# Attention's weight products in three float32r passes instead of seven block products, with every engine's order written out

## The chip, the cores and the metric

The kernel runs on one core of a Trainium2 chip. The metric is the device time of one launch in microseconds, of which the median of several runs is given. TensorE (PE) does the matrix products and writes them to PSUM; VectorE (DVE), ScalarE (ACT) and GpSimd (POOL) work on the data around them; SyncE (SP) issues most of the transfers.

## The reference

The reference is one transformer layer over 4 x 2048 tokens of 256 features in float32: attention within chunks of 32 tokens, then a feed-forward part with 768 hidden features and integer weights.

```python
Q, K, V = x @ W_q.T, x @ W_k.T, x @ W_v.T          # chunks of 32 tokens
S = einsum('bncd,bnkd->bnck', Qc, Kc) * mask       # mask: decay ** (i - j), lower triangle
O = einsum('bnck,bnkd->bncd', S, Vc)
attn = sigmoid(x @ W_g.T) * O @ W_o.T + x
h = layernorm(x + attn)
ffn = (silu(h @ wg.T) * (h @ wu.T)) @ wd.T         # weights: integer / 127
out = layernorm(h + ffn)
```

## The kernel before, in words

The 8192 tokens are cut into 16 blocks of 512 (TB). `W_q.T W_k` is folded once into a matrix m (`make_m`), so a block needs four weight products of 512 tokens by 256 by 256: the gate (g), y = m x, the values (v) and the output projection (o). Scores and values are fp32 products of small pieces (L631, L652). The feed-forward part has six chunks of 128 hidden features (`ffn_up`, L795: fg and fu, each as a float32r high part and an f16 low part, two products per part) and the down projection (`ffn_down`, fdn, L682 or, for the last blocks, chunkwise L858 and L1128).

The four weight products of blocks 1 to 15 (o: 1 to 14) are written in Winograd's form of Strassen: `seven` cuts both operands into quarters and makes seven fp32 products of quarter size instead of eight. The sums of weight quarters are made once (`weight_sums`, POOL), those of token quarters for every block (`token_sums`, POOL, tiles x_sums and go_sums). Four products go first into four banks (p1, p6, p5, p7); ACT copies p1 and p5 out (L505), DVE and POOL build sums of them (L507 to L517); the other three products are accumulated onto three of these banks later (`others`), and ACT and DVE read the quarters out (L524, L530). `feature_major` gives g and y with features on partitions (products of 256 columns), `token_major` gives v and o with tokens on partitions (128 columns).

The loop `for b in range(NB - 2)` works on several blocks at once: the feed-forward part of block b, scores and values and output projection of block n = b + 2, and v, y and g of block m = b + 3. In a steady turn PE does up 0, up 1, scores, up 2, v (first products), up 3, v (rest), values, y (first), up 4, up 5, y (rest), g (first), o (first), g (rest), o (rest), down. The normalised h of block b + 1 is transposed by DVE (`move_h`) and 16 transfers, and split by `split_h`. The layer norm after attention takes the statistics (`moments`, DVE), the root (`root`, ACT, with a table load, and a table load back to silu), a reciprocal on DVE and three small POOL operations (`scale_and_shift`), and `normalize` on ACT.

The order on each engine is that of a planner for instructions left free, and that of the program for those passed to `in_turn` (`tc.keep_in_program_order`). `in_steady_turn` is `in_turn` where the Python flag `steady` is true, which is so for b > 0. Eight PSUM banks are handed out in rotation; the tile pools `sums`, `work` and `xin` have one or two buffers for each tag.

At the head, blocks 0 to 2 have their attention products before the loop begins, and block 0's products are plain fp32 (`attn_gate`, `attn_v`, `attn_y`, `attn_residual`). In block 15 the output projection is also plain fp32 ("pa", L682). A second path for wide integer weights (`wide_block`) is behind a runtime condition and isn't taken with these inputs.

Of the kernel before, what the change touches and what calls it, by code (L numbers as in the profile page):

```python
# [66 lines left out]
HALF = 0.5  # L67
WARM = 512, 512, 128
# [3 lines left out]
def kernel(  # L72
# [130 lines left out]
    def make_m():  # L203
        pm = bank("pm")
        for ec in range(KD):
            for dc in range(KD):
                nc.tensor.matmul(
                    pm[:, ec * D : (ec + 1) * D],
                    lhsT=wq[:, dc, ec * P : (ec + 1) * P],
                    rhs=wk[:, dc, :],  # L210
                    start=(dc == 0),
                    stop=(dc == KD - 1),
                )
        nc.scalar.copy(m_sb.rearrange("p k n -> p (k n)"), pm)
# [3 lines left out]
    nc.scalar.activation(decay, decay, AF.Sigmoid)  # L218
# [10 lines left out]
    power = decay  # L229
    for i in range(CHUNK.bit_length() - 1):  # L230
# [4 lines left out]
        bit = setup.tile([P, CHUNK], F32, tag="bit", name=f"bit_{i}")  # L235
        nc.vector.tensor_copy(bit, bit_int)
        factor = setup.tile([P, CHUNK], F32, tag="factor", name=f"factor_{i}")
        nc.vector.tensor_scalar(factor, bit, -1.0, 1.0, ALU.mult, ALU.add)
        nc.vector.scalar_tensor_tensor(factor, bit, power, factor, ALU.mult, ALU.add)
        nc.vector.tensor_tensor(chunk_mask, chunk_mask, factor, ALU.mult)  # L240
        if i < CHUNK.bit_length() - 2:
            square = const.tile([P, 1], F32, tag=f"power_{i}", name=f"power_{i}")
            nc.vector.tensor_tensor(square, power, power, ALU.mult)
            power = square
    mask = const.tile([P, NG, PAIR], F32, tag="mask", name="mask")
    nc.vector.memset(mask, 0.0)
    for g in range(P // CHUNK):
        rows = slice(g * CHUNK, (g + 1) * CHUNK)
        at = g * CHUNK % PAIR
        nc.vector.tensor_copy(  # L250
            mask[rows, :, at : at + CHUNK],
            chunk_mask[rows, :].unsqueeze(1).to_broadcast([CHUNK, NG, CHUNK]),
        )


# [5 lines left out]
    def integers(w, w_int, name):  # L261
# [6 lines left out]
        for t in both:  # L268
            for i, piece in enumerate(w_int):
                tc.keep_in_program_order(nc.scalar.copy(pieces_of(t, i), piece))  # L270
        return both
# [29 lines left out]
    def in_turn(ins):  # L301
        tc.keep_in_program_order(ins)

# [4 lines left out]
    steady = False  # L308
# [117 lines left out]
    def weight_sums(w, name):  # L426

        a11, a21 = w[:, 0, :P], w[:, 0, P:]
        a12, a22 = w[:, 1, :P], w[:, 1, P:]
# [20 lines left out]
    def feature_major(a, b):  # L450


        def product(i, pb, first, order=free):
# [8 lines left out]
                )  # L462
            )

        return product

    def token_major(a, b):

# [850 lines left out]
```

## Time and profile before

| | us |
|---|---|
| median of 3 runs | 524.97 (523.98 to 525.20) |
| profiled execution: its own time | 525.22 |
| profiled execution: span of the program | 523.6 |
| PE busy | 517.1 |
| DVE, ACT, POOL busy | 327.2, 325.8, 343.3 |
| head: up to the loop's first chunk | 48.8 |
| one steady block | 31.6 |
| block 13 of the loop (b = 13) | 22.8 |

The span runs from the first to the last instruction of the program. In a line of the profile, L813 is a line of the kernel; then come the engine, the operation, and the tiles as out<-in. The records of PE overlap, [...]so their pace is read from the distance of two starts; an fp32 product appears as two records.

### The profile page before, as it was taken

The numbers are of one execution on the slowest core, as the hardware profiler recorded it, in microseconds if no ns is written. First come the engines' busy times: TensorE is split into PE (matmuls) and PEld (weight loads), VectorE is DVE, ScalarE is ACT, GpSimd is POOL, SyncE is SP. The second block draws the span as 40 slices with busy tenths as digits, with TensorE's granted clock in tenths as the row PEclk, the third lists the DMA queues.
The fourth block names the chain that finished last, engine by engine and source line by source line (L and its number), as shares of the span: only waits on it lengthen the run. The fifth ranks groups of instructions, "written<-read, shape, count | busy, mean of one in ns | idle before, by whom it ended". The sixth has DMA issues, their size and how long they took to land.

```text
span 523.6 us, 10506 instructions
## 1 busy us (share of the span) xinstructions
PE 517.1 (99%) x3648; PEld 422.2 (81%) x3648; DVE 327.2 (62%) x867; ACT 325.8 (62%) x646; POOL 343.3 (66%) x475
## 2 busy tenths in 40 slices
PE   9999999999999999999999999999999999999995
PEld 5798887888978789787888878879787888878685
DVE  3868676575655847657475665846657565666554
ACT  3755556475655756667566665756567566666745
POOL 6435875676857768486675866768487685845554
PEclk9999999999999999999999999999999999999999
DMA  7631111212313131121412313131121311102102
GB/s 255 199 109 43 54 51 35 65 41 46 118 28 94 49 114 41 38 85 52 110 42 50 115 25 97 44 111 49 34 89 51 111 42 41 43 20 61 62 21 83
DMA packets 43319, 36.89 MB, mean 70 GB/s; under 512 B 4864, under 2 KB 39168, under 8 KB 43264
## 3 DMA queue, kind: packets, MB, share of 16 engines
q1 hardware_dynamic: 42144, 35.28, 22.9%
q10 hardware_dynamic: 1120, 0.92, 0.6%
q8 instruction: 30, 0.49, 0.4%
q14 instruction: 25, 0.20, 0.1%
HBM read 20.45 MB, written 8.39 MB: 55 GB/s over the span
## 4 chain that ended last, share of the span: by engine, by line
PE 98%; DVE 1%; ACT 0%; issue 0%
PE fg L795 17%; PE fu L795 16%; PE fdn L682 13%; PE p_v L473 9%; PE p_y L455 9%; PE p_g L455 9%; PE p_o L473 8%; PE po L652 5%; PE ps L631 3%; PE fdn L858 2%; PE pa L682 1%; PE pg L571 1%; PE pi L185 1%; PE pv L611 1%; PE py L590 1%; PE fdn L1128 1%
## 5 line engine op out<-in xcount | busy, mean ns | idle before, releaser
L817 POOL TENSOR_TENSOR u_lo<-u,u_hi 128x512 f16<-128x512 f32 (+1 forms) x98 | 122.3, 1256 | 107.0 <-ACT u_hi L816 107.0
L813 DVE SCALAR_TENSOR_TENSOR u<-fu,s 128x512 f32<-128x512 f32 (+1 forms) x98 | 65.2, 677 | 65.5 <-ACT s L803 43.7
L803 ACT ACTIVATE s<-fg 128x512 f32<-128x512 f32 (+1 forms) x98 | 56.6, 584 | 53.5 <-PE fg L795 53.5
L816 ACT CAST u_hi<-u 128x512 fp32r<-128x512 f32 (+1 forms) x98 | 59.5, 610 | 48.5 <-DVE u L813 48.0
L795 PE MATMUL fg<-hT_hi,fg_hi 128*128 128x512 f32 (+1 forms) x196 | 73.8, 458 | 0.0
L795 PE MATMUL fu<-hT_hi,fu_hi 128*128 128x512 f32 (+1 forms) x196 | 60.5, 390 | 0.0
L795 PE MATMUL fg<-hT_lo,fg_lo 128*128 128x512 f16 (+1 forms) x196 | 57.9, 377 | 0.0
L795 PE MATMUL fu<-hT_lo,fu_lo 128*128 128x512 f16 (+1 forms) x196 | 57.4, 375 | 0.0
L682 PE MATMUL fdn<-fd_hi,u_hi 128*128 128x256 f32 x312 | 45.7, 288 | 0.0
L795 PEld LDWEIGHTS fu<-hT_hi,fu_hi 128*128 128x128 f32 x196 | 36.6, 188 | 8.4
L795 PEld LDWEIGHTS fg<-hT_hi,fg_hi 128*128 128x128 f32 x196 | 34.6, 189 | 8.9
L410 ACT ACTIVATE h<-h,shift_h,scale_h 128x256 f32<-128x256 f32 x52 | 27.0, 590 | 22.5 <-POOL shift_h L373 22.5
L682 PEld LDWEIGHTS fdn<-fd_hi,u_hi 128*128 128x128 f32 x312 | 38.9, 189 | 0.3
L682 PE MATMUL fdn<-fd_lo,u_lo 128*128 128x256 f16 x312 | 38.6, 273 | 0.0
L795 PEld LDWEIGHTS <-fu_lo 128*128 128x128 f16 x196 | 19.2, 98 | 22.2
L778 POOL TENSOR_TENSOR hT_lo<-hT,hT_hi 128x512 f16<-128x512 f32 x28 | 35.3, 1279 | 1.2 <-ACT hT_hi L777 1.2
L840 DVE SCALAR_TENSOR_TENSOR r<-fdn,h 128x512 f32<-128x512 f32 x30 | 20.7, 689 | 20.2 <-PE fdn L682 18.1
L795 PEld LDWEIGHTS <-fg_lo 128*128 128x128 f16 x196 | 15.3, 98 | 20.7 <-issue 12.9
L473 PE MATMUL p_v<-v_sums,x_sums 128*128 128x128 f32 x240 | 31.8, 275 | 0.0
L682 PEld LDWEIGHTS <-u_lo 128*128 128x128 f16 x312 | 28.4, 98 | 3.9
L652 PE MATMUL po<-sT,v 128*128 128x128 f32 x256 | 31.2, 275 | 0.0
L455 PE MATMUL p_y<-x_sums,m_sums 128*128 128x256 f32 x120 | 30.8, 379 | 0.0
(211 smaller groups left out, 1154.2 us busy)
## 6 DMA issues: line engine op xcount, KB each, us to landing
x<-in_x_dram SPq DMA_DIRECT2D x16, 512.0 KB, 3.6
xT<-in_xT_dram SPq DMA_DIRECT2D x15, 512.0 KB, 4.2
hT<-sq SPq DMA_DIRECT2D x224, 32.0 KB, 1.9
out_dram<-r SPq DMA_DIRECT2D x13, 512.0 KB, 4.7
out_dram<-r SPq DMA_DIRECT2D x7, 128.0 KB, 1.7
fg_int<-in_ffn_gT_dram SPq DMA_DIRECT2D x3, 256.0 KB, 8.1
fu_int<-in_ffn_uT_dram SPq DMA_DIRECT2D x3, 256.0 KB, 7.1
fd_int<-in_ffn_dT_dram SPq DMA_DIRECT2D x3, 256.0 KB, 5.9
```

Of the source, the lines that this page charges most:

```text
L410: nc.scalar.activation(r[:, g, :], r[:, g, :], AF.Identity, bias=shift[:, g : g + 1], scale=scale[:, g : g + 1],)
L455: nc.tensor.matmul(pb, lhsT=a[i - 1], rhs=b[i - 1], start=first, stop=True, skip_group_check=True,)
L473: nc.tensor.matmul(pb[:, g * P : (g + 1) * P], lhsT=b[i - 1][:, g * P : (g + 1) * P], rhs=a[i - 1], start=first and g == 0, stop=True, ski ...
L652: nc.tensor.matmul(po[:, cols], lhsT=v[:, g, dc * P : (dc + 1) * P], rhs=sT[:, cols], start=True, stop=True,)
L682: nc.tensor.matmul(pb[:, j * D : (j + 1) * D], lhsT=part[:, g * P : (g + 1) * P], rhs=w, start=(i == 0), stop=(i == len(terms) - 1),)
L778: nc.gpsimd.tensor_tensor(in_order[1], whole, in_order[0].bitcast(F32), ALU.subtract)
L795: nc.tensor.matmul(pb, lhsT=w[kind][:, dc, hc * P : (hc + 1) * P], rhs=hT[kind][:, dc, cols], start=(kind == kinds[0] and dc == 0), stop=( ...
L803: order(nc.scalar.activation(s, pg, AF.Silu, scale=SCALE / H_UP))
L813: nc.vector.scalar_tensor_tensor(u, pu, U_UP / H_UP, s, ALU.mult, ALU.mult)
L816: nc.scalar.copy(hi, u)
L817: nc.gpsimd.tensor_tensor(lo, u, hi.bitcast(F32), ALU.subtract)
L840: nc.vector.scalar_tensor_tensor(flat(r, gs), pb, SCALE**2 / U_UP * H_UP, flat(h, gs), ALU.mult, ALU.add)
```

## The change

Each weight product becomes three float32r products. With SHIFT = 2^12, an operand t is split into hi = t * (1 - 0.5/SHIFT), rounded to float32r, lo = t - hi, and a third part, gap. For tokens gap = t - (1 + 1/SHIFT) hi; for weights lo is scaled up by SHIFT after the split and gap = hi - lo. The product is (1 + 1/SHIFT) times the sum of the high and the low product, plus the product of the gaps. `three` runs the high and low pass of both banks, lets ACT multiply each bank by 1 + 1/SHIFT in place in PSUM, and later adds the third pass and finishes the bank: g by ACT's tanh, y by a DVE copy, v by an ACT copy, o by a DVE addition.

The parts of weights are made at the head, hi and the scaling of lo by ACT, lo and gap by POOL. The parts of tokens (x and goT) are made for each block: hi by ACT, lo by POOL, gap by DVE. Block 0 keeps plain fp32. Block 15's output projection is made in three passes too, its third pass between the early and the late terms of the down projection of block 13 (`amid`), and its layer norm goes over POOL's power function and ACT's `normalize`.

`steady` is true from the start, and nearly all instructions of PE, ACT and DVE are pinned to the program's order. The head is rearranged, the casts of the integer weights are spread out between other steps (`cast_fg(0)` and so on), `move_h` comes after chunk 1, the split of h after chunk 5, and in the block without a next one (b = 13) chunk 3 comes behind the values.

```diff
+SHIFT = 2.0**12
+TOP = 1.0 - 0.5 / SHIFT
+WHOLE = 1.0 + 1.0 / SHIFT
...
-    steady = False
+    steady = True
...
+    def weight_parts(w, name, tags):
+        hi, lo = (
+            const.tile([P, KD, D], F32R, tag=tag, name=f"{name}_{kind}")
+            for tag, kind in zip(tags, ("hi", "lo"))
+        )
+        in_turn(nc.scalar.mul(hi, w, TOP))
+        in_turn(nc.gpsimd.tensor_tensor(lo, w, hi.bitcast(F32), ALU.subtract))
+        w_parts[name] = [hi, lo]
+    def weight_up(name):
+        lo = w_parts[name][1]
+        in_turn(nc.scalar.mul(lo, lo.bitcast(F32), SHIFT))
+    def weight_gap(name):
+        hi, lo = w_parts[name]
+        gap = const.tile([P, KD, D], F32R, tag=name, name=f"{name}_gap")
+        in_turn(nc.gpsimd.tensor_tensor(gap, hi.bitcast(F32), lo.bitcast(F32), ALU.subtract))
+        w_parts[name].append(gap)
+    def token_parts(t, name):
+        hi, lo, gap = parts = [
+            sums.tile([P, KD, TB], F32R, tag=f"{name[0]}_{kind}", name=f"{name}_{kind}")
+            for kind in ("hi", "lo", "gap")
+        ]
+        for k in range(KD):
+            whole = hi[:, k, :].bitcast(F32)
+            in_turn(nc.scalar.mul(hi[:, k, :], t[:, k, :], TOP))
+            in_turn(nc.gpsimd.tensor_tensor(lo[:, k, :], t[:, k, :], whole, ALU.subtract))
+        def gaps():
+            for k in range(KD):
+                whole = hi[:, k, :].bitcast(F32)
+                in_turn(nc.vector.scalar_tensor_tensor(
+                        gap[:, k, :], whole, -WHOLE, t[:, k, :], ALU.mult, ALU.add))
+        return parts, gaps
...
+    def three(name, product, finish):
+        banks = [bank(f"p{i}_{name}") for i in range(2)]
+        for i, pb in enumerate(banks):
+            product(i, pb, 0)
+            product(i, pb, 1)
+            in_turn(nc.scalar.mul(pb, pb, WHOLE))
         def others():
...
+            for i, pb in enumerate(banks):
+                product(i, pb, 2)
+                finish(i, pb)
...
+    weight_parts(wg, "wg", ("wg_hi", "wg_lo"))
+    make_mask()
+    weight_parts(wv, "wv", ("wv_hi", "wv_lo"))
+    back_to_silu()
+    sg, gate = attn_gate(0)
+    x_parts, x_gaps = token_parts(xTs[1], "x_1")
...
+    mv = moments(hs[0], "a0", order=in_turn)
+    weight_up("wo")
+    weight_gap("wo")
+    std = root(mv, "a0", HALF, order=in_turn)
+    back_to_silu()
+    v, rest = split_v(2, x_parts)
+    x_gaps()
     goT = attn_values(1, sT_1, v_1, sg_1)
...
         if b:
             normalize(hs[b + 1], *scales_h)
-            moving = move_h(b + 1, hs[b + 1])
-        ffn_up(b, hT, uT, range(0, 1))
+        up_now(b, hT, uT, 0)
         if b == 0:
             g_rest()
-            x_sums = token_sums(xTs[m], f"x_{m}")
-        ffn_up(b, hT, uT, range(1, 2))
+            cast_fd(1)
+            x_parts, x_gaps = token_parts(xTs[m], f"x_{m}")
+        up_now(b, hT, uT, 1)
+        if b:
+            moving = move_h(b + 1, hs[b + 1])
         sT = attn_scores(n, yT)
...
         if more:
-            v_next, v_rest = split_v(m, x_sums)
-        multiply = ffn_up(b, hT, uT, range(3, 4), held=True)
-        if more:
+            v_next, v_rest = split_v(m, x_parts)
+            up_now(b, hT, uT, 3)
             v_rest()
...
         goT = attn_values(n, sT, v, sg)
...
+        go_parts, go_gaps = token_parts(goT, f"go_{n}")
         if more:
-            go_sums = token_sums(goT, f"go_{n}")
-            y_next, y_rest = split_y(m, x_sums)
-        ffn_up(b, hT, uT, range(4, KH))
+            y_next, y_rest = split_y(m, x_parts)
+        else:
+            up_now(b, hT, uT, 3)
+            normalize(r_before, *scales_out)
+            store(b - 2, r_before)
+        up_now(b, hT, uT, 4)
+        go_gaps()
+        up_now(b, hT, uT, 5)
+        hTs[b + 1] = split_h(b + 1, moving)
...
             y_rest()
-            sg_next, g_rest = split_gate(m, x_sums)
-            hs[n], out_rest = split_out(n, go_sums)
+            sg_next, g_rest = split_gate(m, x_parts)
+            hs[n], out_rest = split_out(n, go_parts)
             g_rest()
             mv_h = out_rest()
             ahead = y_next, v_next, sg_next
-            hTs[b + 1] = split_h(b + 1, moving)
+            if m + 1 < NB:
+                x_parts, x_gaps = token_parts(xTs[m + 1], f"x_{m + 1}")
             std_h = root_in_turn(mv_h, of_h, f"h_{b}")
             if b:
                 mv_before, std_before = mv_out, root_in_turn(mv_out, of_out, f"out_{b}")
             back_to_silu()
...
             def between():
-                return scale_and_shift(mv_h, std_h, of_h, f"h_{b}")
+                scales = scale_and_shift(mv_h, std_h, of_h, f"h_{b}")
+                if m + 1 < NB:
+                    x_gaps()
+                return scales
...
         else:
-            hs[n] = attn_residual(n, goT)
-            mv_h = moments(hs[n], f"a{n}", order=in_turn)
             std_out = root_in_turn(mv_out, of_out, f"out_{b}")
-            hTs[b + 1] = split_h(b + 1, moving)
-            std_h = root_in_turn(mv_h, of_h, f"h_{b}")
             back_to_silu()
+            hs[n], out_rest = split_out(n, go_parts)
             scales_out = scale_and_shift(mv_out, std_out, of_out, f"out_{b}")
             normalize(r_before, *scales_out)
             store(b - 1, r_before)
...
-            inverse(std_h, slice(0, NG), HALF)
-            for g in range(NG):
-                scaled(hs[n], g, mv_h, std_h)
-            r_out, mv_out, _ = ffn_down(b, uT, hs.pop(b), chunkwise=True)
+            def amid():
+                return iterated_scale_and_shift(out_rest(), (HALF, 1.0), f"h_{n}")
...
+            r_out, mv_out, scales_h = ffn_down(
+                b, uT, hs.pop(b), chunkwise=True, amid=amid
+            )
+            normalize(hs[n], *scales_h)
             scales_out = iterated_scale_and_shift(mv_out, of_out, f"out_{b + 1}")
```

## The prediction

> **What bounds the kernel now.** I read the page's head and chain first, then the chain in order of time over one steady block, then the engine shares of that block, and last the queues of ScalarE (ACT) and VectorE (DVE) in order of time.
>
> ```profile
> span 523.6 us, 10506 instructions
> PE 517.1 (99%) x3648; PEld 422.2 (81%) x3648; DVE 327.2 (62%) x867; ACT 325.8 (62%) x646; POOL 343.3 (66%) x475
> PE 98%; DVE 1%; ACT 0%; issue 0%
> ```
>
> TensorE (PE) is the end: no other engine holds 2% of the chain. The block that starts at 271.94, in the chain's order of time (start, us, what):
>
> ```profile
> 271.94 0.46 PE fg L795 x2
> ...
> 278.62 1.78 PE p_v L473 x16
> ...
> 282.20 1.34 PE p_v L473 x12
> ...
> 285.33 1.73 PE p_y L455 x8
> ...
> 290.66 1.29 PE p_y L455 x6
> 291.96 1.73 PE p_g L455 x8
> 293.68 1.78 PE p_o L473 x16
> 295.47 1.30 PE p_g L455 x6
> 296.76 1.34 PE p_o L473 x12
> 298.10 5.43 PE fdn L682 x48
> 303.54 0.46 PE fg L795 x2
> ```
>
> One block takes 303.54 - 271.94 = 31.60 us. The four weight products take 3.12 (v), 3.02 (y), 3.03 (g) and 3.12 (o): 12.29 us. In the stages' view of 272.0 to 303.6 ACT is busy 20.1, DVE 19.6 and POOL 21.8 us, so they have slack. How ACT spends a chunk of the feed-forward matters below (ACT's queue: start, length, and in brackets the idle time before it and what ended it):
>
> ```profile
> 256.94 0.60 ACT L803 ACTIVATE s<-fg 128x512 f32<-128x512 f32 x1 [0.78 <-PE fg L795]
> 258.35 0.62 ACT L816 CAST u_hi<-u 128x512 fp32r<-128x512 f32 x1 [0.81 <-DVE u L813]
> 258.88 0.59 ACT L803 ACTIVATE s<-fg 128x512 f32<-128x512 f32 x1
> ```
>
> From one silu to the next is 1.94 us although two operations of 0.6 are in it: ACT waits 0.81 for DVE's multiply between them. In a fixed order that wait is lost.
>
> [...] (DVE and POOL queues):
>
> ```profile
> 10.74 0.24 DVE L239 SCALAR_TENSOR_TENSOR factor<-bit,decay,factor 128x32 f32<-128x32 f32 x1
> 10.89 0.72 POOL L444 TENSOR_TENSOR x_sums<-xT 128x256 f32<-128x256 f32 x1 [0.85 <-DMA xT<-in_xT_dram]
> 10.90 0.76 DVE L239 SCALAR_TENSOR_TENSOR factor<-bit,power,factor 128x32 f32<-128x32 f32 x1
> ```
>
> The same tiny operation takes 0.24 us alone and 0.76 beside a POOL operation, while u (PSUM and SBUF inputs) keeps its 0.69 beside u_lo. [...]
>
> **The change, part by part.**
>
> 1. *PE, products.* A float32r product of 512 columns takes 0.231 us (fg, fu hi: 0.46 for two), one of 256 columns 0.117: fdn's 48 in 5.43 are 24 pairs of 0.226, and its f16 half is 0.110 (twelve f16 in 1.48 = 11 x d + 0.27). After: y and g 12 x 0.231 = 2.77 each, v and o 24 x 0.117 = 2.81 each, 11.16 together. A block saves 12.29 - 11.16 = 1.13 us; the PE's period would be 30.47. Fifteen blocks give 17.0, and the last block's out projection, now 3.46 in fp32 (16 in one piece, "pa"), 0.3 more: 17.3 us if nothing else became late.
>
> 2. *ACT.* Per block it gets 8 in-place scalings PSUM to PSUM 128x512, 4 splits of tokens (float32r out, like hT_hi: 0.51 from start to start), full-width tanh and v copies; it loses the half-width copies of L505 and L524 and the tanh of L552. The scaling isn't in the trace. Bounds: [...] 0.60 (nothing overlapped, hT_hi<-pt is 0.594 long). I take 0.49, the start-to-start of two hT_hi<-pt (1.08 for two). Sum of start-to-start costs: normalisations 8 x 0.49 = 3.9, silu and u_hi 6 x 1.07 = 6.4, scalings 3.9, splits 2.0, h split 1.0, tanh and v 2.0, square roots with table loads 3.4: 22.6; with six waits of 0.87 for DVE (1.94 - 1.07) 27.8 of 30.5 us. So ACT, in a pinned order, is nearly as full as PE.
>
> 3. *The loop through ACT.* Each third pass waits for ACT's scaling, and the next block's ACT work starts with normalisations that wait for this block's third pass. Say the out projection's third pass ends on PE at 0. DVE's second add starts at 0.3, stats 0.61 later; four stats in strict order take 2.25 to the root (479.48 to 481.73 in the last block, already in that order): 3.16. DVE goes on with the residual and two stats, 1.80 (483.78 to 485.58), and the reciprocal at 4.85. POOL's minus, scale, shift follow 0.23 later and normalise starts 0.61 after them: 5.67. But two x gaps follow the reciprocal on DVE. [...] (no row shows a full-size gap; two goT of that size are 0.60 apart, 473.03 and 473.63; below 0 it can't cost, since POOL's chain is serial). POOL waits for one and possibly both: normalise at about 6.65 (between 5.7 and 6.8). From there on ACT: normalise 1.97; chunk 0 1.94; chunk 1 up to u_hi 1.41 (5.33); DVE then does four transposes (1.37) and the mask (0.86) before u of chunk 2, so u_hi 2 is at 8.12, done 8.64; v scalings 0.98; chunk 3 1.94; v copies 0.98; store's normalise 1.97 (14.5); token split 1.02; y scalings 0.98; chunks 4 and 5 3.87 (20.36); h split 1.02; g and o scalings 1.96 (23.3, done 23.4); the last half pass 0.47 and hand-over 0.1: 24.0. The loop is 6.65 + 24.0 = 30.65 us, against PE's 30.47. Period 30.65: 0.95 saved per block, over the 12 periods from block 0 to block 12: **-11.4 us**. PE would wait 0.2 us per block before the out projection's third pass; the down projection is queued behind it, and the adds, the stats and the next normalise hang on both. The pinning itself costs PE nothing else here, since its products are ready when their turn comes.
>
> 4. *Head.* ACT gets the weight splits (4 hi, 4 up), and in order. Where it hurts: root a0 is waited for by ACT (moments now come after the mask product of block 1), then a table load of 1.28, and only then are block 2's v scalings made: about 39.0, third pass of v at 39.6 where PE would be there at 37.9 (1.7 late); the y pass of block 2 waits 0.85 behind three casts; in block 0 two tanh, three casts of fd and the split of x3 stand before silu 1, so PE waits 0.9 for x3's low part and 1.2 for the v scaling. Against it stand 1.7 us of saved products up to 48.8 and 1.1 in block 0. Net **+1.5 us** (from -1 to +3).
>
> 5. *Last blocks.* In block 13 the value products come before chunk 3: they wait 1.2 us for the mask on DVE, which stands behind the transposes. Then ACT has store's normalise (1.97), chunks 4 and 5, h split, the root and two table loads (1.28 each) before the out projection's scaling: it is done at about 23.4 us of the block; PE's early part of the down projection ends at 20.4. PE waits 3.1. The block then takes 26.2 where it took 22.8 (461.5 to 484.3): +3.5. The normalise of block 15 moves from DVE to ACT ahead of chunk 0 of block 14; ACT lags 4 us there, and PE waits about 2 us over transposes, block 15's first chunk and the late down terms. Together **+5.8 us** (from +1 to +8).
>
> 6. *Hidden.* POOL loses 12 half-size operations and gets 4 of full size: 17 of 30.5 us. DVE's 20 us stay under; go's gaps start just after POOL's second go split (0.04 us clear; missed, u of chunk 5 and the loop grow by up to 1.2). PSUM's eight banks: the tightest re-use, o's first bank behind y's copy, has about 0.2 us to spare. SP's loads and stores keep their places near enough, 4 us transfers with over 10 us ahead of need. Memory: the sums' tiles make way for splits.
>
> Sum on the profiled execution: 523.6 + 1.6 outside the span = 525.2; -11.4 + 1.5 + 5.8 = -4.1: 521.1. The median of the runs is 0.25 lower: **521.0** rounded.
>
> **Rivals.**
> - *PE stays the bound* (0.22): [...] POOL's small operations not held up. The period is 30.47 (-13.6), the ends wait less (+3): 514; with free ends 508. For it: PE is 98% of the chain with ACT at 62%. Against it: the 27.8 of 30.5 us.
> - *ACT becomes the bound* (0.20), the slower side: one mechanism, the in-place scaling. Eight a block lie in the loop, so each 0.01 us costs 0.08 a block and 1 us in all. Break-even: the ends cost 7.3, 0.61 a block, so 30.99, that is 0.53 instead of 0.49. At 0.60 the loop is 31.5, the kernel 531; at 0.65, 536. For it: no row shows this form, and ACT would be full. [...]
> - *The ends eat it all* (0.13): period 31.0 with these ends, or 30.65 with the upper ends: 523.5 to 526.5, no change.
> - The likeliest (0.45): 516 to 523.4 by the bounds of 4 and 5, one part PE, one part ACT.
>
> About 0.3% (1.6 us) is what this kernel's measurement can tell from no change. Faster 0.67 (the likeliest and the first rival), same 0.13, slower 0.20. The range that leaves out 2 in 10 is 510 to 531; the likeliest case's own range is 516 to 523.4.
>
> **What would show it.** In the chain: y or g pieces of 1.85 + 0.92, v and o of 1.87 + 0.94 (item 1). PE at 97 to 98% instead of 99, ACT near 80%. Steady period 30.65, idle PE before o's third pass released by ACT; a normalise that starts 6.65 after it. In the waits: POOL minus_h behind DVE's gap. Gaps of 1.7 us near 38 and 3 us in block 13. It is wrong if scalings are spaced over 0.53, if small POOL operations slip between the gaps, or if the ends have no PE idle of this size.

## The result, and the profile after

The changed kernel takes 528.81 us (median of 4 runs, 528.65 to 529.99), the kernel before 524.68 beside it: a ratio of 1.0084 (95% interval 1.0065 to 1.0104). The forecast was 521.0; the sign is wrong. The profiled execution took 528.65 with a span of 527.0, so it stands for the median.

The stages are cut at the first records of the down projections; "forecast" is the difference that the prediction's items gave. Before the change the loop's first chunk begins at 48.56 us; the 48.8 given further up is 0.24 too late.

| stage, us | before | after | difference | forecast |
|---|---|---|---|---|
| start to the loop's first chunk | 48.56 | 51.48 | +2.92 | |
| block 0, to its down projection | 27.82 | 29.91 | +2.09 | +1.5 (with the line above) |
| 12 periods, down of block 0 to 12 | 379.44 | 368.41 | -11.03 | -11.4 |
| down of block 12 to 13 | 22.65 | 22.32 | -0.33 | |
| down of 13 to 14 | 19.03 | 24.89 | +5.86 | |
| down of 14 to 15 | 14.76 | 15.56 | +0.80 | |
| down of 15 to VectorE's last write of r | 7.98 | 8.59 | +0.61 | +5.8 (last four) |
| to the end of the span | 3.34 | 5.78 | +2.44 | 0 |
| sum | 523.6 | 527.0 | +3.4 | -4.1 |

The loop did what was forecast. Of the 7.5 us between -4.1 and +3.4, 3.5 are at the head (its two rows are +5.0 against +1.5), 2.4 behind the last operation, 1.1 in the last blocks (+6.9 against +5.8) and 0.4 in the loop.

The page of the changed kernel: its head, the busy line, the granted clock in 40 slices, the chain by engine.

```profile
span 527.0 us, 9688 instructions
PE 506.6 (96%) x3480; PEld 400.3 (76%) x3480; DVE 312.4 (59%) x730; ACT 379.1 (72%) x705; POOL 286.3 (54%) x313
PEclk9999999999999999999999999999999999998997
PE 78%; DVE 6%; ACT 4%; SPq 3%; issue 2%; POOL 1%; DMA 1%; ACTq 0%; DVEq 0%
```

PE held 98% of the chain before and holds 78% now; the rest is spread over all engines, which means many places and not one new bound. The slice with clock 8 is the 37th, 474 to 487 us: the last blocks.

One steady block in the chain's order of time (start, us, what):

```profile
265.71 5.43 PE fdn L700 x48
...
277.82 1.88 PE p_v L517 x16
...
281.52 1.04 PE p_v L517 x8
...
284.35 1.86 PE p_y L495 x8
...
289.83 0.94 PE p_y L495 x4
290.76 1.84 PE p_g L495 x8
292.61 1.89 PE p_o L517 x16
294.49 0.95 PE p_g L495 x4
295.44 0.94 PE p_o L517 x8
296.39 3.65 PE fdn L700 x32
```

The period is 296.39 - 265.71 = 30.68 here and 30.65 over most blocks. The four products take 11.3 us instead of 12.29. The third pass of v takes 1.04 us in this block where y, g and o take 0.94 or 0.95: TensorE loses 0.1 us there, and its weight loads wait for ACT's scaling of p_v in all 12 periods. How ACT and POOL stand in that block (their queues):

```profile
280.71 1.06 ACT L536 ACTIVATE p_v<-p_v 128x512 f32<-128x512 f32 x2
281.70 0.59 ACT L832 ACTIVATE s<-fg 128x512 f32<-128x512 f32 x1
```

```profile
270.72 0.57 POOL L391 TENSOR_SCALAR minus_h<-rstd_h 128x4 f32<-128x4 f32 x1 [1.67 <-DVE rstd_h L389]
271.25 0.63 POOL L391 TENSOR_SCALAR scale_h<-rstd_h 128x4 f32<-128x4 f32 x1
271.86 0.20 POOL L392 TENSOR_TENSOR shift_h<-mv_a,minus_h 128x4 f32<-128x4 f32 x1
```

Two in-place scalings take 281.70 - 280.71 = 0.99 us from start to start, 0.49 each, the value that was assumed. The small POOL operations, 0.22 us in run 7, take 0.57 and 0.63 beside the two x gaps.

The stall in b = 13 (ACT's queue, then PE's, with the idle time before an instruction in brackets; then that stretch by engine, where the seventh figure is the granted clock):

```profile
475.42 1.28 ACT L350 ACT_TABLE_LOAD   x1
476.72 0.30 ACT L350 ACTIVATE rstd_out<-mv_f,eps 128x4 f32<-128x4 f32 x1
477.03 1.28 ACT L940 ACT_TABLE_LOAD   x1
...
478.44 1.06 ACT L536 ACTIVATE p_o<-p_o 128x512 f32<-128x512 f32 x2
```

```profile
479.07 1.40 PE L517 MATMUL p_o<-wo_gap,go_gap 128*128 128x256 f32 x8 [3.15 <-ACT p_o L536]
480.26 1.06 PE L889 MATMUL fdn<-fd_hi,u_hi 128*128 128x256 f32 x4
```

```profile
472.10:483.50 11.40, 8.24 (x59) 7.24 (x57) 5.17 (x15) 8.52 (x15) 5.87 (x8) 0.85 0.26 86
```

The wait is the 3.1 us of the forecast. What follows was not forecast: four down products take 1.06 us where they take 0.62 in run 3, and the granted clock of the stretch is 0.85.

### The profile page after: what moved, and what is told of

Its sections match the earlier page's. It is cut to its first block, busy times and chain, and to the rows that moved or that the text cites. A ratio compares the mean times of both kernels' runs of the same rounds, so it can differ in the third digit from the quotient of the medians.

```text
span 527.0 us, 9688 instructions
## 1 busy us (share of the span) xinstructions
PE 506.6 (96%) x3480; PEld 400.3 (76%) x3480; DVE 312.4 (59%) x730; ACT 379.1 (72%) x705; POOL 286.3 (54%) x313
## 4 chain that ended last, share of the span: by engine, by line
PE 78%; DVE 6%; ACT 4%; SPq 3%; issue 2%; POOL 1%; DMA 1%; ACTq 0%; DVEq 0%
PE fg L823 15%; PE fu L823 14%; PE fdn L700 12%; PE p_y L495 7%; PE p_o L517 7%; PE p_g L495 7%; PE p_v L517 6%; PE po L669 4%; SPq L788 3%; PE ps L647 3%; DVE u L842 1%; PE fdn L889 1%; DVE st_a L341 1%; DMA hT<-sq 1%; ACT h L429 1%
## 5 line engine op out<-in xcount | busy, mean ns | idle before, releaser
L846 POOL TENSOR_TENSOR u_lo<-u,u_hi 128x512 f16<-128x512 f32 (+1 forms) x98 | 129.4, 1321 | 106.8 <-ACT u_hi L845 106.8
L842 DVE SCALAR_TENSOR_TENSOR u<-fu,s 128x512 f32<-128x512 f32 (+1 forms) x98 | 66.7, 681 | 131.9 <-ACT s L832 111.8
L823 PE MATMUL fg<-hT_hi,fg_hi 128*128 128x512 f32 (+1 forms) x196 | 71.4, 445 | 0.0
L476 POOL TENSOR_TENSOR go_lo<-goT,go_hi 128x512 fp32r<-128x512 f32 x30 | 37.9, 1283 | 30.7 <-ACT go_hi L475 30.7
L476 POOL TENSOR_TENSOR x_lo<-xT,x_hi 128x512 fp32r<-128x512 f32 x30 | 37.8, 1279 | 20.2 <-ACT x_hi L475 20.2
L740 DVE TENSOR_TENSOR h<-p_o,x 128x512 f32<-128x512 f32 x30 | 19.4, 687 | 42.1 <-PE p_o L517 38.5
L669 PEld LDWEIGHTS po<-sT,v 128*128 128x128 f32 x256 | 30.0, 192 | 1.5 <-PE fu L823 1.4
```

The source lines that it names most:

```text
L476: in_turn(nc.gpsimd.tensor_tensor(lo[:, k, :], t[:, k, :], whole, ALU.subtract))
L669: product = nc.tensor.matmul(po[:, cols], lhsT=v[:, g, dc * P : (dc + 1) * P], rhs=sT[:, cols], start=True, stop=True,)
L823: product = nc.tensor.matmul(pb, lhsT=w[kind][:, dc, hc * P : (hc + 1) * P], rhs=hT[kind][:, dc, cols], start=(kind == kinds[0] and dc == ...
L842: nc.vector.scalar_tensor_tensor(u, pu, U_UP / H_UP, s, ALU.mult, ALU.mult)
L846: nc.gpsimd.tensor_tensor(lo, u, hi.bitcast(F32), ALU.subtract)
```

## The experiments

Ratios are against the kernel before, timed beside each run; the changed kernel is 1.0084. Runs 7, 8 and 12 were executed once and have no ratio: only their profiles are read. A diff is against the changed kernel unless said otherwise.

### 1. Without the branch at the end

```diff
-    n_wide = const.tile([1, 1], I32, tag="n_wide", name="n_wide")
...
-    with tc.If(wide_any > 0, preferred_fallthrough_block=False):
...
```

> The changed kernel without its last statement, the condition on the count of wide weights and the path for wide weights behind it (which is not taken with these inputs); nothing else is touched. Theory 1 [...]: TensorE's compare-and-branch takes 3.85 us at the end of the changed kernel's trace, 522.16 to 526.0, although its condition was known before, and the instruction queues carry packets in that time; without the branch the program ends about 1.5 us after its last compute as it would otherwise, so the span is 527.0 - 2.5 to 527.0 - 4 = 523.0 to 524.5, and the time against the kernel before falls from 1.0084 to 1.001 to 1.0035. Rival: the end waits for something else at that place (the last store's landing, 2 us after its issue, or the closing of the program), and the branch only lies beside it: span within 0.5 us of 527.0 and ratio 1.0075 to 1.009.

Ratio 1.0035 (1.0024 to 1.0046), span 524.6. From VectorE's last write of r to the end it is 3.24 us instead of 5.78. The branch is the tail's 2.4 us. What its cost goes with is in run 8.

### 2. The output projection ahead of the root in b = 13

```diff
+            hs[n], out_rest = split_out(n, go_parts)
             std_out = root_in_turn(mv_out, of_out, f"out_{b}")
             back_to_silu()
-            hs[n], out_rest = split_out(n, go_parts)
```

> In the loop's turn b = 13 alone, the high and low pass of the output projection and its two scalings are written ahead of the root (and its two table loads) of the block before. Theory: TensorE's 3.15 us wait for the scaled p_o in that turn comes from ACT's order, with the root and two table loads (3.3 us) ahead of the scalings; they would be made at about 475.5 instead of 479.0, the wait falls below 0.5 us, and the down products behind it run at 0.118 us instead of twice that (1.9 us more): the turn falls by 4.5 to 5.5 us, the ratio to 0.999. Rival A (the wait only moves): the root now comes after the scalings, its normalisation and store later, and block 14's first chunk waits on ACT; 1 us or less is gained, ratio 1.0065 to 1.0085. Rival B: the split of h stands ahead of the scalings and its transfers are late; the wait is still 1.5 to 2 us, ratio about 1.004.

Ratio 1.0034 (1.0019 to 1.0048), span 526.1. The wait is gone and the down projection of block 13 is over after 6.80 us instead of 11.59. But from there to block 14's down projection it is 16.11 us instead of 13.30. ACT's queue says where it went:

```profile
485.42 2.07 ACT L429 ACTIVATE h<-h,term_h,y_h 128x256 f32<-128x256 f32 x4 [2.80 <-POOL term_h L404]
487.40 0.57 ACT L832 ACTIVATE s<-fg 128x512 f32<-128x512 f32 x1
```

ACT stands 2.80 us for block 15's scale, and the silu of block 14's first chunk is behind it. In the changed kernel ACT stands there too, for 4.67 us, but PE arrives late at that place because of its own stall, so it costs nothing. Of the 4.8 us gained, 2.8 moved on: rival A in kind, with less than half of the theory's gain left.

### 3. The wait filled with products

```diff
             def amid():
+                spare = bank("spare")
+                for _ in range(11):
+                    in_turn(nc.tensor.matmul(spare, lhsT=fg[0][:, 0, :P], rhs=hT[0][:, 0, :], start=True, stop=True))
                 return iterated_scale_and_shift(out_rest(), (HALF, 1.0), f"h_{n}")
```

> In the turn b = 13 alone, eleven products of 512 columns (about 2.6 us, into a bank that nothing reads) are added on TensorE ahead of the output projection's third pass, so that they lie in its 3.15 us wait; the wait itself stays. Theory: the slow stretch behind the wait (8 p_o in 1.40 us instead of 0.94, 16 late down products in 3.25 instead of 1.82) is the clock's answer to TensorE's idle time and not a lack of operands: with the idle time filled these take 0.94 and 1.85, 1.9 us are gained although work was added, ratio about 1.005 (1.0045 to 1.0058). Rival: the slow stretch comes from operands or from PSUM in use by other engines; it stays 1.40 and 3.25, and the added products cost 0 to 0.5 us: ratio 1.0084 to 1.0095.

PE's queue, and the stretch by engine:

```profile
478.53 1.22 PE L517 MATMUL p_o<-wo_gap,go_gap 128*128 128x256 f32 x8 [0.60 <-ACT p_o L536]
479.59 0.62 PE L889 MATMUL fdn<-fd_hi,u_hi 128*128 128x256 f32 x4
```

```profile
471.50:481.50 10.00, 9.39 (x71) 8.16 (x70) 3.88 (x9) 8.59 (x15) 5.91 (x7) 1.00 0.19 62
```

The products behind the wait keep their pace, the clock is 1.00, and the down projection of block 13 is over 1.58 us sooner, although 11 products of 0.231 us (2.5 us) were added in it. The time hardly moves, though: ratio 1.0065 (1.0048 to 1.0082), an interval that touches the changed kernel's. Block 14 gives 1.53 back, at ACT, as in run 2. One reservation: in run 4, whose b = 13 is that of the changed kernel, a wait of 3.04 us was followed by the normal pace; in runs 1, 6 and 7 waits of 2.98, 3.16 and 3.04 were followed by the slow one. So a wait of this length was followed by the slow pace in four of five profiled executions. In the changed kernel the granted clock is 1.00 through the wait (475.92 to 479.07 us) and 0.50 from 479.94 to 483.35. Why the wait of run 4 was not followed by this is not shown.

### 4. The mask's chain in PSUM

```diff
-    chunk_mask = const.tile([P, CHUNK], F32, tag="chunk_mask", name="chunk_mask")
+    in_psum = pi.rearrange("p (i c) -> p i c", c=CHUNK)
+    chunk_mask = in_psum[:, 0, :]
...
-                square = const.tile([P, 1], F32, tag=f"power_{i}", name=f"power_{i}")
-                in_turn(nc.vector.tensor_tensor(square, power, power, ALU.mult))
+                square = in_psum[:, 8, i : i + 1]
+                in_turn(nc.vector.tensor_scalar(square, power, power, None, ALU.mult))
```

> The tiles of the mask's chain at the head (the running mask, the factors as they start, the powers of the decay) lie in a PSUM bank instead of SBUF, so that none of these VectorE operations has two SBUF inputs; their number and order stay. Theory [...]: each of these small operations takes 1.2 to 1.3 us in the changed kernel [...]; with a PSUM input they take about 0.2 to 0.25, the mask is done at about 14 us instead of 21.9, the scores of block 0 no longer wait 1.75 us for yT, and the loop's first chunk starts at about 50.1 instead of 51.65 (ratio 1.0055). Rival 1 (chain of ACT): block 0's root stands behind ACT's casts and scalings, so the loop's start moves by less than 0.5 us and the ratio stays 1.0075 to 1.0085. Rival 2 [...]: the small operations stay above 1 us, everything as before.

DVE's queue in the changed kernel, PE's wait that comes of it, and DVE's queue in this run:

```profile
11.88 1.32 DVE L259 SCALAR_TENSOR_TENSOR factor<-bit,power,factor 128x32 f32<-128x32 f32 x1
13.23 1.20 DVE L261 TENSOR_TENSOR chunk_mask<-chunk_mask,factor 128x32 f32<-128x32 f32 x1
14.35 1.28 DVE L264 TENSOR_TENSOR power<-power 128x1 f32<-128x1 f32 x1
```

```profile
22.66 0.34 PE L647 MATMUL ps<-yT,xT 128*64 128x64 f32 x4 [1.49 <-DVE yT L608]
```

```profile
11.24 0.25 DVE L260 SCALAR_TENSOR_TENSOR factor<-bit,pi 128x32 f32<-128x32 f32 x1
11.53 0.20 DVE L262 TENSOR_TENSOR pi<-pi,factor 128x32 f32<-128x32 f32 x1
11.77 0.23 DVE L265 TENSOR_SCALAR pi<-pi 128x1 f32<-128x1 f32 x1
```

In this chain the place of the operand decides: a square of one column, 0.15 us where POOL has no operation (11.70 us), takes 1.28 beside POOL's splits of the weights and 0.23 with its operand in PSUM. The scores' wait is gone. The first chunk starts at 50.56 instead of 51.48, ratio 1.0042 (1.0028 to 1.0056). The 0.5 us that it is later than expected are lost at the next place, the third value pass of block 2, which waits 2.24 us for ACT's scaling (1.75 before) and then runs at half pace (8 products in 1.97 us, 1.23 before).

Part of this head was chance. In runs 1, 3 and 7, which left the head alone, the scores waited for nothing, and the first chunk started at 50.49, 50.96 and 50.85, no later than with the mask in PSUM. In runs 2, 5 and 9, whose head is the same too, it started at 52.70 to 52.97; in run 9 the scores waited 1.98 us, and the value pass behind them took 1.71 us from start to start, where a steady block takes 0.94. The changed kernel's 51.48 is the middle one of these seven. What the mask costs is therefore shown operation by operation, not by the start of the first chunk.

### 5. The ends rearranged, first attempt

```diff
+        else:
+            up_now(b, hT, uT, 3)
         goT = attn_values(n, sT, v, sg)
...
-            normalize(hs[n], *scales_h)
...
-    ffn_up(last - 1, hTs[last - 1], uT, range(0, 1))
-    up(last - 1, uT, 1, 3)
+    up(last - 1, uT, 0, 2)
+    normalize(hs[last], *scales_h)
+    up(last - 1, uT, 2, 3)
```

(The edit of run 2 is also in it.)

> The run before with the out projection's passes ahead of the root gained 4.8 us in the turn b = 13 and lost 2.8 of it in block 14, where ACT stands 2.80 us for block 15's layer norm (its scale comes from GpSimd's power chain) with the first silu behind it. Here, besides that edit, chunk 3 of b = 13 is written ahead of the values again (the values then don't wait for the mask), and block 15's normalise comes after chunk 1 of block 14 instead of ahead of chunk 0. Theory (in a written-out order each of these waits is a matter of place): ACT no longer stands before the first silu; the values' 0.98 us wait is gone; block 14 takes 13.4 to 13.9 us again (16.35 in that run, 13.54 in the changed kernel), the ends give 6 us against the changed kernel, ratio 0.9965 (0.995 to 0.998). Rival (the wait moves on): the transposes of block 15 wait for the later normalise by 2 us or more, or the out projection waits for the later split of goT; block 14 stays above 15 us, ratio 1.001 to 1.0035.

A miss: ratio 1.0128 (1.0101 to 1.0154). From the end of block 13's down projection to block 14's it is 21.15 us. PE's queue, and DVE's:

```profile
490.14 2.81 PE L759 MATMUL pt<-ident,h 128*128 128x128 f32 x8 [4.84 <-ACT h L429]
```

```profile
482.49 0.69 DVE L869 SCALAR_TENSOR_TENSOR r<-fdn,h 128x512 f32<-128x512 f32 x1
...
486.20 0.17 DVE L413 TENSOR_SCALAR v_out<-mv_f 128x4 f32<-128x4 f32 x1
486.31 0.69 DVE L842 SCALAR_TENSOR_TENSOR u<-fu,s 128x512 f32<-128x512 f32 x1
```

Both residuals and their statistics, 482.49 to 486.31, stand ahead of the first u of block 14 on DVE; u_hi follows u on ACT, and the normalise now follows u_hi. The order of one engine was mended and the order of another made it worse.

### 6. Block 2's value scalings ahead of block 0's root

```diff
-    std = root(mv, "a0", HALF, order=in_turn)
-    back_to_silu()
     v, rest = split_v(2, x_parts)
+    std = root(mv, "a0", HALF, order=in_turn)
+    back_to_silu()
```

(On top of run 4's edit.)

> The kernel with the mask's chain in PSUM, and in the head block 2's high and low value pass with its scalings ahead of block 0's root and table load on ACT. With the mask alone in PSUM the scores' wait of 1.75 us went, but the third value pass of block 2 waited 2.24 us instead of 1.75 and then ran at half pace (8 products in 1.97 us instead of 1.23). Theory (ACT's order): the value pass waits under 0.5 us, and block 0's h, which then comes 1 us later, is waited for by its transposes for under 1.2 us; the first chunk of the loop starts at about 48.8 to 49.5 us (50.56 with the mask alone, 51.49 in the changed kernel), ratio 1.0015 (1.000 to 1.003). Rival (the root sets the head): what the value pass gains the transposes of block 0 lose, the first chunk starts within 0.4 us of 50.56 and the ratio is 1.0035 to 1.005.

The first chunk starts at 49.41, as expected; the value pass waits 0.60 (for x's gap) and the transposes 1.10 in two pieces. The ratio, 1.0039 (1.0025 to 1.0054), does not show it against run 4: in this profile the slow stretch of b = 13 is there (that down projection takes 11.41 us), in run 4's it isn't (9.92). The theory is right at its place; the time alone would not have told.

### 7. The gaps of x behind the down projection

```diff
             def between():
-                scales = scale_and_shift(mv_h, std_h, of_h, f"h_{b}")
-                if m + 1 < NB:
-                    x_gaps()
-                return scales
+                return scale_and_shift(mv_h, std_h, of_h, f"h_{b}")
...
             r_out, mv_out, scales_h = ffn_down(b, uT, hs.pop(b), between)
+            if m + 1 < NB:
+                x_gaps()
```

> In the loop the two gaps of x on VectorE are moved from between the halves of the down projection to behind its second half, so that GpSimd's minus, scale and shift of the layer norm are not held up by them (570 and 631 ns instead of 220 for two of these in the changed kernel). Theory of the forecast (the loop through ACT sets the period): the small operations take 220 ns each, normalise starts about 0.7 us earlier after the out projection, and the period goes from 30.65 to TensorE's own 30.47 to 30.52 us, 1.6 to 2.2 us less between block 0 and block 12. Rival (TensorE's period is 30.65 for other reasons, such as small waits of its third passes that have nothing to do with the layer norm): the period stays within 0.04 of 30.65, although normalise is earlier.

```profile
269.62 0.22 POOL L391 TENSOR_SCALAR minus_h<-rstd_h 128x4 f32<-128x4 f32 x1 [2.07 <-DVE rstd_h L389]
269.81 0.22 POOL L391 TENSOR_SCALAR scale_h<-rstd_h 128x4 f32<-128x4 f32 x1
```

POOL's queue: the small operations are back at 0.22. The period is 30.55 from block 2 on, 0.10 less, and 1.39 us over the 12. The outcome lies between the two: the loop through ACT did set the period, but only by 0.10. The 0.10 us is the one at v's third pass, which takes 0.94 here in every period.

### 8. TensorE's code moved by 128 instructions

```diff
+    for _ in range(64):
+        nc.tensor.matmul(
+            pi[:, :2],
+            lhsT=nc.const_aps.tensor(0.0, [P, P]).bitcast(F32R),
+            rhs=nc.const_aps.tensor(0.0, [P, 2]).bitcast(F32R),
+            start=True,
+            stop=True,
+        )
```

> The changed kernel with 64 more products of two columns (nothing reads them) among the warm-up products at the head, so that all later TensorE code lies 128 instructions further on in memory; the path for wide weights and the branch stay. Its own time is not of interest (the head may lose up to 6 us), only the branch at the end. Theory [...]: TensorE's compare-and-branch takes 0.4 us as in the kernel before, and the program ends 1.4 to 2.5 us after the last VectorE operation where it was 5.8. Rival [...]: it stays at 3.8 us.

PE's sequencer at the branch, two compare-and-branch instructions (shortest, median, longest in ns), in the kernel before, after and in this run:

```profile
L1257 PEldq COMPARE_BRANCH  x2: 95/252/410, 520.9 to 521.2; - x2
```

```profile
L1329 PEldq COMPARE_BRANCH  x2: 95/1972/3850, 521.9 to 522.2; - x2
```

```profile
L1338 PEldq COMPARE_BRANCH  x2: 95/202/310, 534.7 to 535.0; - x2
```

The branch is the same, and so is the path that it jumps over; only the place of the code differs. It costs 0.31 us here and 3.85 in the changed kernel, 3.54 us apart. In the changed kernel and in runs 5, 6, 7, 9 and 10 the span ends 8.0 to 8.3 us after the last down product, in the kernel before and in run 11 5.5. One more thing differs between the kernels before and after: on the queue that the page calls "q8 instruction" a packet starts at 523.1 us in the changed kernel, about 1 us into the branch, and none in the 8 us ahead of it; in the kernel before one starts at 515.8, 5.4 us ahead of the branch. What these packets hold, and whether the branch waits for one, the traces do not show. Run 10 moved the code by 72 instructions and run 3 by 22: no effect.

### 9. The ends laid out for each engine

```diff
-            std_out = root_in_turn(mv_out, of_out, f"out_{b}")
-            back_to_silu()
+            scales_out = iterated_scale_and_shift(mv_out, of_out, f"out_{b}")
             hs[n], out_rest = split_out(n, go_parts)
...
+            def between():
+                up_now(b + 1, hTs[b + 1], uT_next, 0)
...
+    multiply = ffn_up(last - 1, hTs[last - 1], uT, range(1, 2), held=True)
+    normalize(hs[last], *got["h"])
+    multiply()
```

(Also chunk 3 ahead of the values, as in run 5, and block 15's transposes behind chunk 3.)

> The last rearrangement of the ends failed on VectorE: in its order the residual and statistics of b = 13's down projection (3.5 us) stood between block 15's statistics and the first u of block 14, and ACT's in-order u_hi and normalise behind that u; the transposes then waited 4.84 us. Here only the ends of the changed kernel are edited, and the order is laid out for each engine: chunk 3 of b = 13 ahead of the values; the scale of block 12's output from GpSimd's power function instead of ACT's root (two table loads and a reciprocal less); block 14's chunk 0 between the two halves of the late down products, so that its u stands between the two residuals; block 15's normalise behind the silu of chunk 1, its transposes behind chunk 3. Theory (each end wait is a place in some engine's order): no TensorE wait above 0.6 us from b = 13 on, from the down projection of block 12 to that of block 14 40.5 to 42.5 us (47.2 in the changed kernel, 41.7 in the kernel before), ratio 0.996 to 0.999. Rival (the work of the ends doesn't fit ACT and VectorE in any order, so waits only move): 44 us or more, ratio above 1.002.

Ratio 0.9978 (0.9971 to 0.9985). The largest PE wait from b = 13 on is 0.41 us, and from the down projection of block 12 to that of 14 it is 42.8 us instead of 47.2. With the ends alone mended, the change is faster than the kernel before, by 0.2%.

### 10. All edits, with padding

```diff
-WARM = 512, 512, 128
+WARM = 512,
...
+    pad(16, pi)
...
+    pad(24, bank("pad"))
```

(And the edits of runs 4, 6, 7 and 9; in block 0 the split of x ahead of the casts of fd. `pad` issues products of two columns.)

> All of it together: the ends laid out by engine, the mask's chain in PSUM, block 2's value scalings ahead of block 0's root, the gaps of x behind the second half of the down projection, in block 0 the split of x ahead of the casts of fd, and 72 instructions more on TensorE where it is idle (16 two-column products for two of the warm-up products, 24 behind the last product), to move the branch. Theory (the slowdown is the sum of separate places, and the loop's gain is real): 2.3 us from the head, 1.0 from block 0, 1.3 from the loop, 6 from the ends, against the changed kernel, ratio 0.9885 to 0.992; with the branch at 0.4 us 2.4 us more, 0.984 to 0.9875. Rival (the waits belong together: ACT and VectorE are full in these stretches and what goes at one place comes back at the next): half of the sum or less, ratio 0.995 or more.

Ratio 0.9979 (0.9969 to 0.9988): no better than run 9, and the branch still 3.8 us. PE's queue at the head:

```profile
2.06 4.19 PE L201 MATMUL pi<-const-float32-0.0 128*128 128x2 f32 x16
6.11 6.18 PE L596 MATMUL pg<-xT,wg 128*128 128x512 f32 x8
```

The eight gate products take 6.18 us, 3.86 in the changed kernel, and start at 6.11 instead of 4.97: ahead of them stands the padding, which took the place of two of the three wide warm-up products. By its ratio this is the rival's outcome, but the loop (30.57), the ends and the head behind that point are as the theory had them; what ate the gain is the experiment's own cost, which run 11 takes away.

### 11. All edits, without padding

```diff
+                n = 2 if kind == 2 and to_halve else 1
...
+                for c in range(0, TB, TB // n):
...
-                        pb,
+                            pb[:, c : c + TB // n],
...
-                        rhs=b[kind][:, k, :],
+                            rhs=b[kind][:, k, c : c + TB // n],
...
```

(For the first 64 such products; in block 0 the low casts of fd behind the value pass.)

> All edits together as in the run before, with two changes. The 24 and 16 tiny products are gone and the warm-up is the old one: in that run they took 4.19 us for 16 and the eight products behind them ran at half pace (6.18 us instead of 3.8), 3.5 us lost. In their place 64 third-pass products of 512 columns (y and g of the first blocks) are issued as two of 256, which moves the branch by 128 instructions at 0.003 us each. And in block 0 the low casts of fd stand behind the value pass (with the casts right behind the split of x the scaling of v was waited for 1.59 us). Theory: the head is 3.5 us shorter than in the run before (loop's first chunk at 49.4), block 0 takes 28 to 29 us instead of 29.9, the branch 0.3 to 0.4 us instead of 3.8: together 516 to 518.5, ratio 0.984 to 0.989. Rival 1 (the padding wasn't what made the head late): no gain there, about 520. Rival 2 (the branch's cost isn't a matter of where the code lies): it stays at 3.8 us and the time at 518.5 to 520.5.

**517.98 us, ratio 0.987 (0.9853 to 0.9886): 1.3% faster than the kernel before and the best version here.** The page:

```profile
span 516.8 us, 9832 instructions
PE 504.2 (98%) x3544; PEld 403.7 (78%) x3544; DVE 306.4 (59%) x730; ACT 377.2 (73%) x701; POOL 278.7 (54%) x317
PE 84%; DVE 5%; ACT 4%; SPq 3%; issue 2%; DMA 1%; POOL 0%; DVEq 0%; ACTq 0%
```

The first chunk starts at 49.41, the branch takes 0.30, the tail 3.32. Block 0 did not move (29.91): its value pass no longer waits 0.92 us for its scaling, but a wait of 1.70 us for the scaling of g came in its place. Against the kernel before, the loop's 12 periods give 12.0 us, head and block 0 still cost 2.9 and the last blocks 2.3.

### 12. Without the in-place scalings

```diff
-            in_turn(nc.scalar.mul(pb, pb, WHOLE))
```

> The changed kernel with the in-place scalings of the product banks on ACT left out everywhere (the products then lack the factor 1 + 1/4096 on their high and low parts, so this part of the computation is missing); the order of everything else stays. The kernel with the gaps moved away showed a period of 30.55 to 30.57 us instead of 30.65; open is what holds it above TensorE's sum of 30.47. Theory (ACT is in the way): 3.9 us a block less on ACT, no third pass waits, the period is 30.46 to 30.50, 1.9 to 2.3 us less between block 0 and block 12 than the changed kernel; in b = 13 the 3.15 us wait and the half pace behind it are gone; in the head the value pass of block 2 still waits for nothing but its operands. Rival (TensorE's own sum is larger than the forecast had it[...]): the period stays at 30.55 or above, although ACT is a sixth emptier.

```profile
278.36 0.94 PE p_v L517 x8
...
292.17 0.94 PE p_o L517 x8
```

The period is 30.55 from block 2 on, the same as in run 7. This is the rival's outcome: with 3.9 us less on ACT nothing is gained over run 7, so PE's own sum is 30.55 and not 30.47; the passes start 1.88, 0.94 (y), 1.84, 0.92 (g), 1.88, 0.94 (v), 1.89, 0.94 (o) apart, 11.23 instead of 11.16. The span is 519.9, 7 us under the changed kernel's: 2.6 at the head and in block 0, 1.5 in the loop, 3.0 from the down projection of block 13 to that of 14.

## Why the prediction was wrong, step by step

**Item 1 (PE's products): right.** 30.55 against 30.47; 0.07 of the difference is in the passes (run 12).

**Item 2 (the scaling): right.** 0.49 us each from start to start, as taken; the operation lasts 0.56 to 0.57 us, where hT_hi<-pt, of the same size but written to SBUF, lasts 0.60, so the write to PSUM is the shorter one here. The slower rival, which hung on this cost, did not come true, though the result is on its side.

**Item 3 (the loop): right in time, wrong in part in its reason.** 30.65 was forecast and measured, the gain 11.03 against 11.4. POOL's small operations are held up beside the gaps (0.57 and 0.63 us, 0.22 in run 7), and normalise starts 272.09 - 265.71 = 6.38 us after the out projection (6.65 forecast). But of the 0.18 us that the loop was to stand above PE's sum, only 0.10 is this loop (run 7, run 12); the rest is PE's own sum, so that the forecast's exact period is in part luck. Nor does PE wait where the forecast had it, before the out projection's third pass: that pass takes 0.94 us in the changed kernel and in run 12. PE waits before v's third pass (1.04 against 0.94), 9 us after normalise, because the scaling of v stands behind ACT's first three chunks. The second half of the 24.0 us that the forecast laid out on ACT does not hold PE up. (In run 1, whose loop is the same, the period is 30.69 and v's third pass takes 0.93; where that execution loses its tenth is open.)

**Item 4 (the head): the step that failed most, +5.0 against +1.5, above its upper bound of +3.** The other six executions with the same head give +4.0 to +6.5. The sum itself slips: its own terms, 1.7 + 0.85 + 0.9 + 1.2 - 1.7 - 1.1, make +1.85. It priced most of what it named well: the root a0 and the value pass behind it (1.75 against 1.7), block 0's waits for x's low part (1.07 against 0.9) and for the v scaling (0.92 against 1.2); the 0.85 for the y pass did not come (0.2 at most). It left the mask out. The prediction quoted the very lines that show VectorE slowed beside POOL (the mask's operation at 0.24 and 0.76), then counted with such a delay in the loop only; at the head the change puts full-size splits of the weights on POOL, 1.27 us each, beside the same chain of small operations, and pins the yT copies behind that chain. The scores waited 1.49 us (1.75 for their weight loads). The scaling of block 0's h took 3.34 us for four operations, most of it beside POOL's split of goT from 42.26 us on (in the kernel before three take 1.46), and its transposes waited 0.43. The waits named here are 5.7 us; less the 2.8 of saved products that is 2.9 of the 5.0. The rest lies in passes around these waits that ran longer than elsewhere (v's high and low passes in block 0's turn take 3.88 us from start to start, 2.08 in a steady block) and is not taken apart further.

**Item 5 (the last blocks): +6.9 against +5.8; the waits right, two terms wrong.** The 3.15 us wait for the out projection's scaling was forecast at 3.1, the values' wait at 1.2 (0.96). The half pace behind the wait, 1.6 us by run 3, was not forecast. Nor was a wait in the down projections of the last two blocks, 0.6 and 0.3 us for POOL's u_lo, of the 1.4 us that those stages grew. Waits of 2.98 to 3.16 us were followed by half pace in four of five profiled executions (run 3). And the 2 us expected of ACT's lag in block 14 were only latent: PE's stall gave ACT the time. Run 2 took the stall away and there they were, 2.8 us. That the sum came within 1.1 us is therefore in part luck: what it left out (1.6 and 0.9) is about as much as it counted and did not come (2).

**Item 6 and the frame of the sum: 2.4 us missing.** The 3.3 us between the last VectorE operation and the end of the span were carried over as constant, without a word. The branch took 0.41 us in the kernel before, 3.85 in the changed one and 0.31 with PE's code moved by 128 instructions (run 8); the change moved that code too.

**The rivals.** "The ends eat it all" was the nearest: it had the loop at 30.65 and the ends at their upper bound. Its upper bounds, 3 for the head and 8 for the ends, together give 524.8; with the measured head of 5.0 and a tail of 2.4 it would have been on the slower side. The slower case was given one mechanism inside the loop; what made the kernel slower lay wholly outside it.

## What to carry to other kernels

When every engine's order is written out, price the head and the last blocks engine by engine like a steady block, and ask of each wait that is to go which engine it was giving time to: run 2 lost half of its gain and run 5 more than all of it to waits that the first wait had hidden. A slowing of one engine beside another (0.24 to 0.76 us in the prediction's own lines) or a clock drop (0.50 behind the wait in b = 13) that is seen in one stage has to be looked for in every stage where the same kinds of operation meet. Before believing a loss of some microseconds at the very end, look at the branch (0.31 to 3.85 us here). What the same products would take with the planner's order at the head and the ends was not tried.

## What was unexpected of the hardware

- The branch over the path for wide weights took 0.41 us in the kernel before, 3.85 in the changed kernel and 0.31 with TensorE's code moved by 128 instructions (run 8; run 11 agrees with 0.30).
- Behind products of two columns the next products are slow: in run 8 64 of them take 10.80 us from start to start, and the eight products behind them 6.65 instead of 3.86; in run 10 16 take 4.05 and the eight behind them 6.18.
- VectorE operations of 32 columns, and of one, take 1.2 to 1.3 us each, six in a row in the changed kernel, beside GpSimd's full-size operations of 1.25 to 1.29, and 0.20 to 0.25 with an operand in PSUM (run 4).
- Like waits of about 3 us do or do not cost half pace behind them: 2.98 to 3.16 us in the changed kernel and in runs 1, 6 and 7 did, 3.04 in run 4 did not. In the changed kernel the granted clock is 0.50 from 479.94 to 483.35 us, behind a wait that ended at 479.07.
